# Normalising the second batch inside the first output projection of an attention and feed-forward block

## The chip, the cores and the metric

The kernel runs on one core of a Trainium2 chip. A core has five engines, each with an instruction queue of its own that runs in order: TensorE (PE, matrix products and transposes, written to PSUM), VectorE (DVE), ScalarE (ACT), GpSimd (POOL) and SyncE (SP, which here only issues DMA transfers). PE's weight loads have a row of their own (PEld). All transfers share 16 DMA engines. The metric is the device time of one execution in microseconds (us), lower is better.

## The reference

The input x has 2 batches of 1024 tokens of 1024 values; 32 query heads of 32 values share 8 key/value heads, so four query heads (a group) use one key head. The feed-forward weights are 4-bit numbers, packed eight to a word, with zero points and scales per group of 128 rows.

```python
xn = _layernorm(x, axis=-1)                     # (x - mean) / sqrt(var + 1e-5)
q, k, v = xn @ wq, xn @ wk, xn @ wv             # per head
q, k = _apply_rope(q), _apply_rope(k)           # pairs of values turned by the token's angle
attn = softmax(q @ k.T / sqrt(32) + causal mask)
s = (attn @ v) @ wo
h = silu(xn @ w_gate) * (xn @ w_up)             # w = scale * (nibble - zero - 1)
g = silu(h @ w_down)
out = x + s * g
```

## The kernel before

The work is done in five kinds of stage: for each of the two batches norm, projection, attention and output projection, and after both the feed-forward part. Everything is in fp32; a product is done as two instructions in the profile.

**Norm** (`norm`, L299). The tokens are taken in eight tiles of 128 (`t`). SP loads a tile `xt` of 512 KB, VectorE computes mean and variance (`bn_stats` twice, `bn_aggr`), ScalarE the square root (`std`), VectorE the reciprocal and the normalised `xn`; PE turns `xn` in eight 128x128 transposes into two PSUM tiles `ps_ln`, and ScalarE copies these into `xnT` (channels on partitions, tokens along the free axis). Three `xt`, three `xn` and four `ps_ln` buffers exist. The pools are opened inside the function and closed at its end.

**Projection** (`project`, L321). `turned` multiplies one 128-column weight tile with all eight channel slices of `xnT`, for each half of 512 tokens (`n`): 16 PE instructions into `ps_qk`. VectorE, POOL and ScalarE turn the result by the token angles (`cs`, `rot`) and split it into two parts, `hi` and `lo`, which SP writes to DRAM (`ks`, `qs`). First come the two key tiles `c`, each for both halves, then eight query tiles, then the values (`values`, L363) for eight token tiles. Beside the queries the row maxima of the first key head's scores are computed (`Maxima`, `head.rows()`, L477), and each channel slice of `xnT` is split and stored for the feed-forward part (`xs`). In batch 0, `look` (L209) checks and prepares the 4-bit tables in between.

**Attention** (`attend`, L554) runs under a manual schedule: the engines get its instructions in the order in which they are traced. A step is one key tile of 128 for one group `g` and one half of the queries `qb`. PE computes scores into four PSUM tiles `st`, ScalarE exponentiates them into `p`, POOL masks the diagonal tiles (`affine_select`, L636), PE multiplies `p` with the values (`o`, L655). The sums of the weights (`l`, L673) are products with ones; to save PE work POOL first adds several `p` tiles together (L757, and L783 for what is left after the last step). `groups` (L588) says which: pairs for full tiles, and all four diagonal tiles into one. The maxima of later heads are woven in by a planner with costs (`Clock`, `turn`). Query stacks live in three sets and key stacks in four, loaded by SP one or more heads ahead.

**Output projection** (`project_out`, L785). The eight weight tiles `w_o` are loaded first. For each block of 256 tokens PE computes all eight column tiles into one PSUM tile `ps_wo` of four banks (two buffers, so all eight banks). VectorE copies the first half of the columns back into `oT` and ScalarE the second half, and SP writes the block to `sT` in DRAM. Before each column tile three steps of `unpack` (L234) are traced: the 4-bit weights are loaded (`qw`, `zt`), nibbles taken apart on VectorE, turned to fp32 on ScalarE (`nf`, two buffers) and written to DRAM by POOL's queue (`ng`, 512 KB per write, 22 MB in batch 0). Steps that are left follow after the loop.

**What sets the order.** Outside attention and the down projection, the framework plans the order of each engine's queue ahead of time: by priority, which is the order of tracing, among the instructions that a model of the hardware holds ready. On the chip each queue then runs in that order and waits by semaphores. Memory for a pool is reused after earlier pools on the same stack are closed; a pool with `reuse_waits="tile"` waits for the single tiles that lay there, another for the earlier pool as a whole. The main loop over batches is at L1308.

Of the kernel before, what the change touches and what calls it, by code (L numbers as in the profile page):

```python
# [10 lines left out]
F32 = mybir.dt.float32  # L11
# [12 lines left out]
P = 128  # L24
# [12 lines left out]
def block_kernel(  # L37
# [261 lines left out]
    def norm(b, xnT):  # L299
        with tc.tile_pool(name="ln", bufs=3) as pool, tc.tile_pool(name="ln_ps", bufs=4, space=PSUM) as psp:  # L300
            for t in range(NT):
                xt = pool.tile([P, D], F32, name="xt")
                nc.sync.dma_start(xt, x[b, t * P : (t + 1) * P, :])
                stats = pool.tile([P, 2, 6], F32, name="stats")
                for h in range(2):
                    nc.vector.bn_stats(stats[:, h, :], xt[:, h * 512 : (h + 1) * 512])
                mv = pool.tile([P, 2], F32, name="mv")
                nc.vector.bn_aggr(mv, stats.rearrange("p h s -> p (h s)"))
                std = pool.tile([P, 1], F32, name="std")
                nc.scalar.activation(std, mv[:, 1:2], AF.Sqrt, bias=eps)  # L310
                rstd = pool.tile([P, 1], F32, name="rstd")
                nc.vector.reciprocal(rstd, std)
                xn = pool.tile([P, D], F32, name="xn")
                nc.vector.tensor_scalar(xn, xt, mv[:, 0:1], rstd, ALU.subtract, ALU.mult)
                for h in range(NS // 4):
                    ps = psp.tile([P, 4, P], F32, name="ps_ln")
                    for j in range(4):
                        nc.tensor.transpose(ps[:, j, :], xn[:, (4 * h + j) * P : (4 * h + j + 1) * P], ident)
                    nc.scalar.copy(xnT[:, 4 * h : 4 * h + 4, t * P : (t + 1) * P], ps)  # L319

    def project(b, xnT, qs, ks, v, side, head):  # L321


        with tc.tile_pool(name="qkv_w", bufs=3) as wp, tc.tile_pool(name="qkv", bufs=3) as pool, tc.tile_pool(
            name="qkv_t", bufs=1
        ) as tp, tc.tile_pool(name="qkv_ps", bufs=3, space=PSUM) as psp, tc.tile_pool(
            name="v_ps", bufs=2, space=PSUM
        ) as vps, tc.tile_pool(name="x_split", bufs=2) as xp:
# [5 lines left out]
            def load(w_dram, c):  # L334
                w = wp.tile([P, NS, P], F32, name="w_qk")
                nc.sync.dma_start(
                    w, w_dram.rearrange("(g p) n -> p g n", p=P)[:, :, c * P : (c + 1) * P]
                )
                return w

            def turned(w, dst, work=iter(())):
                for n in range(NB):
# [27 lines left out]

            wanted = [(wk, c) for c in range(2)] + [(wq, c) for c in range(NC)]
            loaded = [load(*wanted.pop(0)) for _ in range(2)]
            w = tp.tile([P, NS, N_KV * HD], F32, name="w_v")
            nc.sync.dma_start(w, wv.rearrange("(g p) n -> p g n", p=P))

            def following():
                if wanted:
                    loaded.append(load(*wanted.pop(0)))
                return loaded.pop(0)

            for c in range(2):
                turned(following(), ks[c])
# [55 lines left out]
    class Maxima:  # L438


        def __init__(self, qs, ks, pool, ps):
# [112 lines left out]
    def attend(head, v, oT):  # L554
# [5 lines left out]
        with ExitStack() as st:  # L560
# [27 lines left out]
            def groups(qb):  # L588
                full = [[k, k + 1] for k in range(0, qb * QB, 2)]
                return full + [list(range(qb * QB, (qb + 1) * QB))]  # L590
# [803 lines left out]
```

## Time and profile before

| | us |
|---|---|
| median of 3 runs | 2343.35 (2342.94 to 2345.72) |
| the profiled execution | 2346.94 |
| its span, first to last instruction | 2345.2 |
| PE busy | 2254.8 (96%) |
| VectorE, ScalarE, POOL busy | 1410.5, 1130.3, 801.6 |
| mean granted PE clock | 0.982 of full speed |

The stages, by PE's first and last instructions in the trace: norm of batch 0 until 32.5 us, projection until 223.6, attention until 559.4, output projection with the unpacking until 671.5, norm of batch 1 until 707.8, projection until about 890, attention until 1223.5, output projection until 1336, then the feed-forward part.

In a row of the timeline the columns are start, length, engine, line, operation, output and inputs, partitions and elements, and count; in brackets stands how long the engine was idle before it and what it waited for. In a row of stretches the columns are the stretch and its length, the busy time of PE, PEld, DVE, ACT and POOL with counts, the granted PE clock, the share of the DMA engines and GB/s. In a row of waits stand who waited for whom, the sum, the count and the longest.

### The profile page before, as it was taken

To read this page: it belongs to the slowest core of one execution; us is meant where nothing else is said; L and a number is where in the kernel's file an instruction comes from. 1 tells how busy PE (TensorE), PEld (TensorE's weight loads), DVE (VectorE), ACT (ScalarE), POOL (GpSimd) and SP (SyncE) were. 2 spreads that over 40 slices of the span, in tenths; PEclk is the share of its full clock that TensorE was granted. 3 is DMA by queue.
4 is the path that set the end of the run, shared out by engine and by line. 5 is a ranking of instruction groups with operands and counts; after the bars stand their busy time and mean duration, and the time that the engine had idled before them with its cause. 6 is when DMAs were issued, how large, how long until landed. Compare 5 with 4: busy or idle time off the path is not lost.

```text
span 2345.2 us, 30574 instructions
## 1 busy us (share of the span) xinstructions
PE 2254.8 (96%) x11265; PEld 1553.5 (66%) x11265; DVE 1410.5 (60%) x2244; ACT 1130.3 (48%) x1795; POOL 801.6 (34%) x561
## 2 busy tenths in 40 slices
PE   6999999998969999999989999999999999999987
PEld 4446555555854455555548878888877888888765
DVE  6362777762244545777722266767777677767775
ACT  3012544544332004444532365565787655556775
POOL 1421777785312325777670000000234100001352
PEclk8999999999989999999999999999999999999999
DMA  6645122105977434222029622322646645323464
GB/s 225 206 158 162 46 67 69 37 22 170 310 232 260 133 98 108 49 61 67 1 68 323 188 70 68 81 58 78 259 144 221 183 131 148 94 69 109 151 204 149
DMA packets 262342, 309.49 MB, mean 132 GB/s; under 512 B 18283, under 2 KB 202987, under 8 KB 262040
## 3 DMA queue, kind: packets, MB, share of 16 engines
q1 hardware_dynamic: 250964, 269.00, 38.5%
q0 software_dynamic: 9472, 33.83, 4.6%
q10 hardware_dynamic: 1748, 4.62, 0.7%
q8 instruction: 91, 1.49, 0.3%
q14 instruction: 67, 0.55, 0.1%
HBM read 214.58 MB, written 97.03 MB: 133 GB/s over the span
## 4 chain that ended last, share of the span: by engine, by line
PE 77%; issue 9%; POOL 8%; DVE 2%; DMA 2%; ACT 2%; SPq 0%; POOLq 0%; DVEq 0%
PE acc L1069 27%; PE acc L952 11%; PE ps_wo L799 10%; PE st L608 7%; PE s L503 7%; PE o L655 5%; PE ps_v L366 2%; PE l L673 2%; PE st L623 2%; POOL rot L353 2%; POOL rot L354 2%; PE ps_qk L346 2%; DMA xt<-in_L_attn_x 1%; POOL p L757 1%; PE s L497 1%
## 5 line engine op out<-in xcount | busy, mean ns | idle before, releaser
L1069 PE MATMUL acc<-x,w 128*128 128x512 f32 x2752 | 640.2, 393 | 1.5 <-ACT gate L1040 0.9
L1069 PEld LDWEIGHTS acc<-x,w 128*128 128x128 f32 x2752 | 512.3, 188 | 121.0 <-DVE h L1042 6.9
L513 DVE TENSOR_REDUCE mx<-s 128x1 f32<-128x512 f32 (+3 forms) x672 | 384.0, 608 | 202.0 <-PE s L503 111.3
L841 DVE TENSOR_SCALAR acc<-acc,r_gu 128x1024 f32<-128x1024 f32 x301 | 389.1, 1293 | 160.5 <-PE acc L1069 158.2
L633 ACT ACTIVATE p<-st 128x512 f32<-128x512 f32 (+3 forms) x768 | 314.7, 497 | 310.7 <-PE st L623 285.0
L839 ACT ACTIVATE acc<-acc,r_gu 128x1024 f32<-128x1024 f32 x301 | 327.5, 1088 | 230.1 <-PE acc L1069 225.2
L1053 POOL TENSOR_TENSOR h_lo<-h,h_hi 128x512 fp32r<-128x512 f32 x78 | 100.3, 1287 | 819.4 <-ACT h_hi L1052 440.5
L757 POOL TENSOR_TENSOR p<-p 128x1536 f32<-128x1536 f32 (+3 forms) x124 | 367.3, 2966 | 8.3 <-ACT p L633 6.9
L503 PE MATMUL s<-kst,qst 128*128 128x512 f32 (+3 forms) x768 | 295.0, 414 | 5.0 <-DVE mx L513 4.8
L346 PE MATMUL ps_qk<-xnT,w_qk 128*128 128x512 f32 x640 | 295.0, 603 | 0.7 <-ACT xnT L319 0.7
L841 DVE TENSOR_SCALAR acc<-acc,r_d 128x512 f32<-128x512 f32 x320 | 241.6, 759 | 67.1 <-PE acc L952 64.6
L608 PE MATMUL st<-qst,kst 128*128 128x512 f32 (+3 forms) x768 | 246.9, 379 | 5.0 <-ACT p L633 4.6
L839 ACT ACTIVATE acc<-acc,r_d 128x512 f32<-128x512 f32 x320 | 210.8, 662 | 65.6 <-PE acc L952 58.7
L952 PE MATMUL acc<-h_lo,w 128*128 128x512 f32 (+1 forms) x576 | 228.9, 397 | 2.9 <-POOL h_lo L1053 2.6
L952 PE MATMUL acc<-h_hi,w 128*128 128x512 f32 (+1 forms) x576 | 229.5, 398 | 0.7 <-ACT h_hi L1052 0.7
L799 PE MATMUL ps_wo<-oT,w_o 128*128 128x256 f32 x1024 | 224.9, 383 | 0.0
L503 PEld LDWEIGHTS s<-kst,qst 128*128 128x128 f32 x768 | 138.6, 189 | 129.9 <-DVE mx L513 68.2
L799 PEld LDWEIGHTS ps_wo<-oT,w_o 128*128 128x128 f32 x1024 | 196.7, 192 | 30.2 <-issue 2.9
L346 PEld LDWEIGHTS ps_qk<-xnT,w_qk 128*128 128x128 f32 x640 | 118.7, 192 | 123.3 <-issue 119.5
L608 PEld LDWEIGHTS st<-qst,kst 128*128 128x128 f32 x768 | 130.5, 189 | 66.5 <-ACT p L633 55.8
L655 PE MATMUL o<-p,v 128*32 128x512 f32 (+3 forms) x1536 | 164.4, 500 | 10.4 <-POOL p L636 10.4
L356 ACT CAST rot_hi<-rot 128x512 fp32r<-128x512 f32 x40 | 24.6, 617 | 269.8 <-POOL rot L354 240.3
(149 smaller groups left out, 1986.3 us busy)
## 6 DMA issues: line engine op xcount, KB each, us to landing
w<-ng SPq DMA_DIRECT2D x86, 512.0 KB, 6.0
qst<-qs SPq DMA_DIRECT2D x256, 128.0 KB, 3.9
w<-nd SPq DMA_DIRECT2D x63, 512.0 KB, 3.7
ng<-nf POOLq DMA_DIRECT2D x42, 512.0 KB, 6.1
x<-xs SPq DMA_DIRECT2D x32, 512.0 KB, 5.8
xt<-in_L_attn_x SPq DMA_DIRECT2D x16, 512.0 KB
w_qk<-in_L_attn_wq SPq DMA_DIRECT2D x16, 512.0 KB, 4.6
xs<-x_hi SPq DMA_DIRECT2D x16, 512.0 KB, 3.2
```

What stands on the lines that cost most here:

```text
L346: nc.tensor.matmul(ps, w[:, s, :], xnT[:, s, tok], start=(s == 0), stop=(s == NS - 1))
L503: nc.tensor.matmul(s[:, c * w : (c + 1) * w], q[j][:, qt * P : (qt + 1) * P], k[:, k0:k1], start=n == 1, stop=c == n - 1 and (n > 1 or not ...
L513: nc.vector.tensor_reduce(mx[:, at, js[0] : js[0] + n, k0 // TB], s[:, : w * n].rearrange("p (j t) -> p j t", j=n), AX.X, ALU.max)
L608: nc.tensor.matmul(s[:, q0:], kst[g][:, kt * P : (kt + 1) * P], stack[g][j][:, qlo + q0 : qlo + TB], start=True, stop=False,)
L633: nc.scalar.activation(p[:, j, q0:], st[j][:, q0:], AF.Exp, scale=1.0 / math.sqrt(HD))
L655: nc.tensor.matmul(o[HD * j : HD * (j + 1), q0:], v[:, kt, HD * g : HD * (g + 1)], p[:, j, q0:], start=(kt == 0), stop=last,)
L757: what(*args)
L799: nc.tensor.matmul(ps[:, c, :], ws[c][:, g, :], oT[:, g, t0 : t0 + BLK], start=(g == 0), stop=(g == NS - 1))
L839: nc.scalar.mul(a, a, r)
L841: nc.vector.tensor_scalar(a, a, r, None, ALU.mult)
L952: nc.tensor.matmul(acc[c], w[:k, c * P : (c + 1) * P], ht[:k, :], start=(f == 0 and t == 0), stop=(t == 1), skip_group_check=(f > 0),)
L1069: nc.tensor.matmul(a[:, n, :], w[i][:, g * P : (g + 1) * P], xs[t][:, g, n * TB : (n + 1) * TB], start=(g == 0 and t == 0), stop=(t == 1), ...
```

## The change

The norm becomes a generator that does one token tile at a time, with pools given by the caller. For batch 0 it runs ahead as before, now with eight `xt` buffers. For batch 1 it runs inside the output projection of batch 0: after every half of the columns of a block one tile of 128 tokens is traced, with three `xt` buffers and two `ps_ln`; the transposes are ordered behind the first half's last product. The output projection uses PSUM tiles of half the columns (two banks, three buffers), copies them by turns with VectorE and ScalarE into separate tiles `wo_r` (three buffers), and writes these to `sT` from POOL's and ScalarE's queues. `xnT` is opened before the output projection and closed before attention.

Both key tiles come as one weight `w_k` of 1 MB, loaded after the fourth token tile in batch 0 and after the last output weight for batch 1; the value weight is later loaded into the same tile. The keys are projected for the first 512 tokens (both tiles) and then for the last. In the last group's second half the four diagonal tiles are no longer added by POOL; each is summed by PE on its own. Most pools wait by tile, the first key and query stacks get a pool of their own at the bottom, and the stacks are placed in another order in memory.

```diff
-    def norm(b, xnT):
-        with tc.tile_pool(name="ln", bufs=3) as pool, tc.tile_pool(name="ln_ps", bufs=4, space=PSUM) as psp:
-            for t in range(NT):
-                xt = pool.tile([P, D], F32, name="xt")
+    def norm(b, xnT, pool, psp, bufs):
+        for t in range(NT):
+            xt = pool.tile([P, D], F32, name="xt", bufs=bufs)
...
+                nc.scalar.copy(xnT[:, 4 * h : 4 * h + 4, t * P : (t + 1) * P], ps)
+            yield
+    def load_w_at(pool, w_dram, c, **kw):
+        w = pool.tile([P, NS, P], F32, **{"name": "w_qk", **kw})
+        return w, nc.sync.dma_start(w, w_dram.rearrange("(g p) n -> p g n", p=P)[:, :, c * P : (c + 1) * P])
+    def load_kv(pool, w_dram, w=None):
+        if w is None:
+            w = pool.tile([P, NS, N_KV * HD], F32, name="w_kv")
+        nc.sync.dma_start(w, w_dram.rearrange("(g p) n -> p g n", p=P))
+        return w
...
-            for c in range(2):
-                turned(following(), ks[c])
+            for n in range(NB):
+                for c in range(2):
+                    turned(w_k[:, :, c * P : (c + 1) * P], ks[c], blocks=[n])
+            w = load_kv(None, wv, w_k)
             head.keys()
...
-            keys = [head.k] + [kp.tile([P, T], F32R, name=f"kst_{i}") for i in range(1, 4)]
+            keys = {0: head.k, **{i: kp.tile([P, T], F32R, name=f"kst_{i}") for i in (1, 3, 2)}}
...
-            sets = [head.q] + [[qp.tile([P, T], F32R, name=f"qst_{i}_{j}") for j in range(NREP)] for i in (1, 2)]
+            sets = {0: head.q, **{i: [qp.tile([P, T], F32R, name=f"qst_{i}_{j}") for j in range(NREP)] for i in (2, 1)}}
...
-            def groups(qb):
+            def groups(g, qb):
                 full = [[k, k + 1] for k in range(0, qb * QB, 2)]
-                return full + [list(range(qb * QB, (qb + 1) * QB))]
+                diag = list(range(qb * QB, (qb + 1) * QB))
+                return full + ([[k] for k in diag] if g == NKV - 1 and qb == NB - 1 else [diag])
...
-                    n = len(groups(qb)) - 1 - groups(qb).index(grp)
+                    n = min(2, len(groups(g, qb)) - 1 - groups(g, qb).index(grp))
...
-                    at(end + 4 - n, total, hd, hd["p"], span(qb, grp[0]), grp[0] == 0, last)
+                    at(max(i + 3, end + 4 - n), total, hd, hd["p"], span(qb, grp[0]), grp[0] == 0, last)
...
-    def project_out(b, oT, side, turns):
+    def project_out(b, oT, side, turns, xnT, xp):
         BLK = 256
+        HC = NC // 2
+        with ExitStack() as st:
+            wp = st.enter_context(tc.tile_pool(name="wo", bufs=NC, reuse_waits="tile"))
+            res = st.enter_context(tc.tile_pool(name="wo_out", bufs=3, reuse_waits="tile"))
+            psp = st.enter_context(tc.tile_pool(name="wo_ps", bufs=3, space=PSUM, reuse_waits="tile"))
+            following = iter(())
+            if xnT is not None:
+                ln = st.enter_context(tc.tile_pool(name="ln", bufs=3, reuse_waits="tile"))
+                ln_ps = st.enter_context(tc.tile_pool(name="ln_ps", bufs=2, space=PSUM, reuse_waits="tile"))
+                following = norm(b + 1, xnT, ln, ln_ps, 3)
+            loads = [load_w_at(wp, wo, c, name="w_o") for c in range(NC)]
+            ws = [w for w, _ in loads]
+            w_k = None
+            if xp is not None:
+                with tc.issue_after(loads[-1][1].ins):
+                    w_k = load_kv(xp, wk)
+            first = None
             for t0 in range(0, T, BLK):
...
+                for h in range(2):
+                    ps = psp.tile([P, HC, BLK], F32, name="ps_wo")
+                    for c in range(HC):
+                        for _ in range(turns):
+                            next(side, None)
+                        for g in range(NS):
+                            mm = nc.tensor.matmul(
...
+                    first = first or mm
+                    with tc.issue_after(first.ins):
+                        next(following, None)
+                    r = res.tile([P, HC, BLK], F32, name="wo_r")
+                    copy, queue = ((nc.vector.tensor_copy, nc.gpsimd), (nc.scalar.copy, nc.scalar))[h]
+                    copy(r, ps)
+                    queue.dma_start(sT_dram[b][:, HC * h : HC * (h + 1), t0 : t0 + BLK], r)
+            return w_k
...
+    x_open, xnT, xp = open_x()
+    with tc.tile_pool(name="ln", bufs=3) as ln, tc.tile_pool(name="ln_ps", bufs=4, space=PSUM) as ln_ps:
+        for t, _ in enumerate(norm(0, xnT, ln, ln_ps, NT)):
+            if t == NT // 2 - 1:
+                w_k = load_kv(xp, wk)
     for b in range(B):
...
+            room = [q0p.tile([P, T], F32R, name=f"st_{j}") for j in range(1 + NREP)]
...
+                x_open.close()
                 attend(head, v, oT)
+        if b == B - 1:
+            ffn_args = start_ffn(ffn_open)
+            xnT = xp = None
+        else:
+            x_open, xnT, xp = open_x()
+        with tc.tile_pool(name="unpack", bufs=2, side="right", reuse_waits="tile") as up:
+            side = unpack(up, b)
+            w_k = project_out(b, oT, side, 3, xnT, xp)
+            for _ in side:
+                pass
```

## The prediction

> **What bounds the kernel now.** I read the page's engine rows and slices first, then busy time by stretch, then the chain of waits and the engines' timelines around the places that the change touches.
>
> ```profile
> PE 2254.8 (96%) x11265; PEld 1553.5 (66%) x11265; DVE 1410.5 (60%) x2244; ACT 1130.3 (48%) x1795; POOL 801.6 (34%) x561
> ```
> TensorE (PE) is busy for 96% of the span, so a gain must come from the 90 us in which it is idle or at a low clock. Stretches (span of the stretch, then PE, PEld, DVE, ACT, POOL busy, PE clock, DMA share, GB/s):
>
> ```profile
> 24.00:28.00 4.00, 1.69 (x8) 1.29 (x7) 2.87 (x7) 1.95 (x4) 0.00 (x0) 0.73 1.09 321
> 672.00:680.00 8.00, 0.00 (x0) 0.00 (x0) 0.74 (x1) 2.29 (x2) 0.00 (x0) 0.67 0.98 278
> 700.00:704.00 4.00, 1.92 (x10) 1.55 (x9) 3.02 (x8) 1.66 (x4) 0.00 (x0) 0.50 0.00 0
> 559.40:615.60 56.20, 56.20 (x258) 49.28 (x255) 19.17 (x57) 23.13 (x24) 18.92 (x22) 0.98 0.91 276
> 615.60:671.40 55.80, 55.80 (x260) 49.03 (x259) 12.45 (x38) 22.97 (x24) 20.13 (x26) 1.00 0.95 286
> ```
> The two norms (first three rows) leave PE idle at half clock. Beside the first output projection (last two) PE has no idle time, VectorE is idle 72% and ScalarE 59% of it, but the DMA engines are 91 to 95% busy with the unpacking. PE's timeline at the end of attention, in the second norm and at the first product:
>
> ```profile
> 32.50 27.94 PE L346 MATMUL ps_qk<-xnT,w_qk 128*128 128x512 f32 x60 [0.68 <-ACT xnT L319]
> 550.30 1.08 PE L655 MATMUL o<-p,v 128*32 128x256 f32 x8 [3.75 <-POOL p L636]
> 551.16 1.94 PE L673 MATMUL l<-p,ones_f 128*32 128x512 f32 x8
> 558.07 1.42 PE L673 MATMUL l<-p,ones_f 128*32 128x512 f32 x8 [2.84 <-POOL p L783]
> 684.80 3.65 PE L318 MATMUL ps_ln<-ident,xn 128*128 128x128 f32 x16 [13.09 <-DVE rstd L312]
> 707.78 5.48 PE L366 MATMUL ps_v<-w_v,xnT 128*128 128x256 f32 x14 [0.68 <-ACT xnT L319]
> ```
> And the chain of waits, where one group of 16 product instructions at full clock can be read:
> ```profile
> 671.90 10.32 DMA xt<-in_L_attn_x
> 713.26 6.87 PE ps_qk L346 x16
> ```
> Last, how far ScalarE runs behind PE in the output projection, by its PSUM copies, and why:
> ```profile
> 629.41 0.99 ACT L805 COPY oT<-ps_wo 128x1024 f32<-128x1024 f32 x1
> 668.20 0.99 ACT L805 COPY oT<-ps_wo 128x1024 f32<-128x1024 f32 x1
> ACT nf L259 <- DMA ng<-nf: 56.5, 19, 6.0
> ```
> A block of 256 tokens takes PE 28.0 us (112.0 / 4), so blocks 2 and 3 were complete at 615.5 and 643.5; their copies came 13.9 and 24.7 us later, because they stand in ScalarE's queue behind unpack conversions that wait for `ng` writes. PE doesn't feel it: it has two block buffers.
>
> **The second norm moved.** Between the end of the output projection (671.5) and the first key product (713.1) pass 41.6 us. Of PE's work there 64 transposes move into the projection, at 27.7 / 128 = 0.216 us each (page's group of L318): 13.8 us. The 14 value instructions of 707.78 come back at the end of the stage at full rate, 24.62 / 114 = 0.216 each: 3.0 us. What goes is 41.6 - 13.8 - 3.0 = **24.8 us**: the wait for x (10.3 us behind the last unpack writes), the VectorE chain, and the half clock.
>
> What moves with it: eight x loads and a 1 MB key weight on SP's queue, past the unpack's qw and zt loads, some 0.4 us of issue each, hidden as SP is mostly waiting. x3 to x7 wait for a buffer of three, which gives them about three halves (42 us) of lead over their transposes; even the 10.3 us landing fits. Per tile VectorE takes 1.29 + 0.21 + 0.15 + 0.81 = 2.5 us, 20 us in all, and ScalarE 8 x (0.3 + 1.2) + 1.3 table load = 13 us; both fit the idle time. The writes of sT leave SP for POOL (0.9 us each by its `ng` issues) and ScalarE's queue. The new `wo_r` buffers add a wait of copies for the sT write three halves earlier: 42 us against a landing of 11.0 us, so nothing, unless ScalarE is over 30 us late. The value weight now waits on SP for the last key product, with the rotated keys' writes behind it; it is needed over 120 us later. I put these at nothing.
>
> **What takes its place.** The transposes stand in PE's queue between two halves, and all later products stand behind them. They wait for two PSUM tiles (`ln_ps` has two buffers, one tile of tokens needs both), so transposes of tile i+1 wait until ScalarE has copied tile i, 14.0 us of PE time earlier. But ScalarE's queue is 13.9 us late at the middle and 24.7 us at three quarters. With 14 us of tolerance the stall is 24.7 - 14.0 = 10.7 us if the lag stays as it was; the lag grew by 10.8 us in 28, and if the planner puts the unpack 15.7 us (one half and its transposes) later, it reaches 24.7 + 6.1 = 30.8 and the stall 16.8. I take the middle, **13.8 us**, since more DMA traffic (5.2 MB at 281 GB/s is 18 us) speaks for growth and the earlier loads of w_o (below) against it. The ends are 0 (the planner orders norms ahead of conversions) and 60 (third rival).
>
> A stall also costs clock. After the idle 1.1 us at 225.2 PE ran at 0.50 from 228 to 234, and after the 2.84 us at 555.2 until 562. Inside the stall that only lets ScalarE catch up; after the last one about 4 us at half rate are lost, **2.0 us**.
>
> The Trainium skill, TensorE: Matmul & The Clock Gate, section Why this matters for your kernels, says the clock is kept as long as no idle gap exceeds some 3 us. The rows above show drops after shorter gaps; by the rule three stalls of under 3 us each would cost no clock, and the forecast would be 2 us lower.
>
> **The start.** Before, the first key product starts at 32.5, after all eight tiles; the fourth group ends at 32.5 + 9.07 (chain; half clock) + 3 x 6.87 = 62.2. After, eight x buffers let all loads go at once. The first lands at 4.3 (first VectorE work); 512 KB at the 320 to 370 GB/s seen from 24 to 32 us is 1.6 us, so tile 3 lands near 9 and w_k near 12.5. VectorE then sets the pace: tile 3 leaves it at 4.3 + 4 x 2.5 + 0.9 (round trip to ScalarE) = 15.2, transposes and copy about 2.2: the first product at 17.4. PE then owes four groups (27.5), 32 transposes (6.9) and 2.2 for the half clock: 54.0. Tile 7 leaves VectorE at 25, in time. Gain **8.2 us**. If the first group's PSUM bank is only free after the last tile, it starts at about 27.3 and ends at 57.0: 5.2. With no half clock: 10.4. A loss has no mechanism here: the same loads come earlier; 0 is the floor.
>
> **The tails of attention.** Of the three POOL sums over the diagonal p tiles of the last head (3.45 + 2.36 + 1.27 us) none is left; PE gets three more groups of `l` (384, 256, 128 columns). The first tail still starts at 550.3, behind the 4.51 us POOL sum of a full pair. Then at half clock o 0.86, l 1.71, l 1.71 to 554.6, and at full clock 0.89 + 0.66 + 0.21 + 0.44 + 0.22: 557.0 instead of 559.4, and 2.6 us at half clock behind it (1.3 us) are gone: 3.7. The second tail, from 1213.9, ends at 1220.1 instead of 1223.5, and 1.4 of clock: 4.8. Sum 8.5, floor 0 (a late w_o); I take **8.0**. Those output weights now lie first on the query set last used by head 6, so part of their 4 MB can land before 545, out of the busy stage.
>
> **Half columns** in the second output projection: PE waited 0.52 us at 1338.2 for ScalarE's copy, which waited for VectorE's of the same tile. Separate tiles: **0.5**. Key order, memory order of stacks and the finer waits elsewhere: PE lost under 6 us in the first projection (0.81 + 1.96 + 1.41 + 1.53), to row maxima, which the change leaves as they are: 0.
>
> **Sum.** 24.8 + 8.2 + 8.0 + 0.5 - 13.8 - 2.0 = 25.7 us. The profiled execution took 2346.94 us (span 2345.2), 3.6 above the median of 2343.35; from it the sum gives 2321.2, from the median 2317.7. I forecast 2318.
>
> **Rivals.** (1) No coupling: norms and copies stay ahead of ScalarE's lag, nothing for stalls and clock: 25.7 + 15.8 = 41.5, so 2302. For: the idle time of VectorE and ScalarE; against: the 24.7 us lag. (2) The start doesn't move, since the first group waits for the last tile or for w_k, and the tails give only half: 2343.35 - (24.8 + 4 + 0.5 - 15.8) = 2330. For: DMA and VectorE are full there; against: the first group has no use for tiles 4 to 7. (3) Slower: VectorE's queue waits for x inside the unpack. Each x took 10.3 us to land at 671.9 where about 5 are usual (4.92 for the next); if each of eight holds the nibble work 5.4 us, ScalarE's lag grows by 43, the stall to 57. Then 41.5 - 57 - 2 = -17.5: 2361. It decides when the stall passes 39.5 us, 2.9 times my value. For: DMA at 95%; against: loads with three buffers of lead.
>
> **Chances.** My forecast (2308 to 2324) 0.45; rival 1 0.22; rival 2 0.15; rival 3 0.13; between it and rival 2, within 0.2% (4.7 us, about what can be told from no change), 0.05. So faster 0.82, same 0.05, slower 0.13. The range runs from rival 1 with the best start, 2300, to a stall of 30 us with rival 2's start, 2339.
>
> **What would show it.** First product L346 near 17 instead of 32.5; no PE wait for POOL L783; no idle time between ps_wo and ps_qk of batch 1; waits of ps_ln in the output projection put down to ScalarE's xnT copies, 14 us in sum; PE in that stage 112 + 14 busy. I am wrong if those waits are missing or pass 30 us, or if the unpack's tail holds the rotations afterwards.

## The result, and the profile after

The changed kernel takes 2349.68 us (median of 14 runs, 2346.70 to 2353.04) against 2343.14 us of the kernel before (14 runs beside them, 2340.69 to 2345.97): a ratio of 1.0027, 95% interval 1.0019 to 1.0035. It is slower by 0.27%, where 2318 us was forecast. The two profiled executions lie apart from these medians on opposite sides (before 2346.94 us, above all 14; after 2347.66 us, near the lowest; span 2345.9), so that the traces have to explain a loss of 0.7 us, not of 6.5. Against the forecast gain of 25.7 us, 26 us are missing by the traces and 32 by the medians. One execution of one run below, the one with the old tail, is left out of its ratio: it took 3634.33 us, at a mean granted clock of 0.556.

PE's row of the page after, and its group for the output projections, which had no idle time before (columns: busy, mean ns, idle ahead of it and what ended most of that):

```profile
PE 2249.7 (96%) x11313; PEld 1550.2 (66%) x11313; DVE 1410.3 (60%) x2244; ACT 1131.3 (48%) x1797; POOL 795.5 (34%) x563
L822 PE MATMUL ps_wo<-oT,w_o 128*128 128x256 f32 x1024 | 227.7, 384 | 23.5 <-DMA w_o<-in_L_attn_wo 23.5
```

The new wait is 23.5 us for the output weights. PE's timeline after, at the start, in the first output projection, and in the second:

```profile
27.49 27.77 PE L354 MATMUL ps_qk<-xnT,w_kv 128*128 128x512 f32 x64
...
548.86 3.72 PE L822 MATMUL ps_wo<-oT,w_o 128*128 128x256 f32 x16
...
630.78 1.97 PE L318 MATMUL ps_ln<-ident,xn 128*128 128x128 f32 x8 [8.48 <-ACT xnT L319]
649.93 1.14 PE L318 MATMUL ps_ln<-ident,xn 128*128 128x128 f32 x8 [2.02 <-ACT xnT L319]
669.94 1.97 PE L318 MATMUL ps_ln<-ident,xn 128*128 128x128 f32 x8 [5.06 <-ACT xnT L319]
686.98 27.63 PE L354 MATMUL ps_qk<-xnT,w_kv 128*128 128x512 f32 x64
```
```profile
1194.16 1.08 PE L665 MATMUL o<-p,v 128*32 128x256 f32 x8 [3.74 <-POOL p L646]
1200.96 3.72 PE L822 MATMUL ps_wo<-oT,w_o 128*128 128x256 f32 x16
1205.68 7.17 PE L822 MATMUL ps_wo<-oT,w_o 128*128 128x256 f32 x32 [1.00 <-DMA w_o<-in_L_attn_wo]
1235.04 102.60 PE L822 MATMUL ps_wo<-oT,w_o 128*128 128x256 f32 x464 [22.18 <-DMA w_o<-in_L_attn_wo]
1337.29 3.12 PE L1100 MATMUL acc<-x,w 128*128 128x512 f32 x12
```

Up to 1200.96 the change gains about what was forecast: the second output projection starts 22.55 us earlier than before (1223.51). Then PE does 48 of its 512 product instructions and stands for 22.18 us. The feed-forward part starts at 1337.29, before at 1335.97. In the stretches of that stage after, PE is empty while the DMA engines are fully busy (columns as in the forecast's rows of stretches):

```profile
1205.68:1212.85 7.17, 7.17 (x32) 6.00 (x32) 0.00 (x0) 0.00 (x0) 0.00 (x0) 1.00 1.00 384
1212.85:1235.04 22.19, 0.01 (x2) 0.01 (x1) 0.00 (x0) 0.00 (x0) 0.00 (x0) 0.56 1.09 364
1235.04:1337.30 102.26, 102.26 (x465) 89.62 (x465) 19.36 (x52) 26.75 (x27) 13.45 (x16) 0.98 0.66 206
```

What the DMA engines carried is on SP's queue. Before:

```profile
1185.85 24.62 SPq L791 DMA_DIRECT2D w_o<-in_L_attn_wo  x5
1226.42 14.50 SPq L819 DMA_DIRECT2D x<-xs  x16
1241.92 8.89 SPq L810 DMA_DIRECT2D w<-ng  x3
1250.87 5.21 SPq L791 DMA_DIRECT2D w_o<-in_L_attn_wo  x3
```

And after, with SP's longest wait in that stretch:

```profile
1079.52 122.03 SPq L327 DMA_DIRECT2D w_o<-in_L_attn_wo  x3
1203.86 13.91 SPq L850 DMA_DIRECT2D x<-xs  x16
1218.73 8.94 SPq L841 DMA_DIRECT2D w<-ng  x3
1227.72 8.82 SPq L327 DMA_DIRECT2D w_o<-in_L_attn_wo  x5
```
```profile
SPq L327 <- PE l L683: 120.8, 1, 120.8
```

The first of these rows merges three loads: the first is issued at 1079.5, and SP then waits 120.8 us, until attention's last product with the values `v` ends at 1200.4, before it issues the second and third. The loads behind them wait in the same queue. There the 16 transfers of x for the feed-forward part (8 MB) and three of its weights (1.5 MB) come next, and the other five output weights only from 1227.72. Before, five of the eight had been issued ahead of x. In the built program of after, the buffers of the second and third weight lie on `v`, which attention reads until its last product; before, `v` lay below the weights and shared no byte with them. The traces show no addresses, but they fit: the last scores, which read the key and query stacks, end at 1189.5, so the stacks are not what SP waits for until 1200.5. The first output projection shows the same wait without the harm: SP issues one weight at 504.1, waits 44.2 us and issues the other seven from 548.4, but there no x goes ahead of them, and PE waits only 0.33 us.

### The profile page after: what moved, and what is told of

It reads as the page before. It is cut to its first block, busy times and chain, and to the rows that moved or that the text cites. A ratio compares the mean times of both kernels' runs of the same rounds, so it can differ in the third digit from the quotient of the medians.

```text
span 2345.9 us, 30638 instructions
## 1 busy us (share of the span) xinstructions
PE 2249.7 (96%) x11313; PEld 1550.2 (66%) x11313; DVE 1410.3 (60%) x2244; ACT 1131.3 (48%) x1797; POOL 795.5 (34%) x563
## 4 chain that ended last, share of the span: by engine, by line
PE 72%; issue 9%; POOL 8%; DMA 5%; ACT 2%; DVE 2%; SPq 1%; ACTq 0%; POOLq 0%; DVEq 0%
PE acc L1100 27%; PE acc L983 12%; PE s L510 7%; PE st L618 7%; PE o L665 5%; PE ps_wo L822 5%; PE l L683 3%; POOL rot L361 2%; PE st L633 2%; POOL rot L362 2%; DMA ng<-nf 2%; PE ps_v L374 1%; PE ps_qk L354 1%; POOL p L767 1%; PE s L504 1%
## 5 line engine op out<-in xcount | busy, mean ns | idle before, releaser
L767 POOL TENSOR_TENSOR p<-p 128x2048 f32<-128x2048 f32 (+3 forms) x122 | 360.3, 2958 | 8.3 <-ACT p L643 6.9
L822 PE MATMUL ps_wo<-oT,w_o 128*128 128x256 f32 x1024 | 227.7, 384 | 23.5 <-DMA w_o<-in_L_attn_wo 23.5
L354 PE MATMUL ps_qk<-xnT,w_qk 128*128 128x512 f32 x512 | 237.6, 600 | 0.0
L665 PE MATMUL o<-p,v 128*32 128x512 f32 (+3 forms) x1536 | 164.1, 499 | 10.4 <-POOL p L646 10.4
L354 PEld LDWEIGHTS ps_qk<-xnT,w_qk 128*128 128x128 f32 x512 | 93.7, 191 | 91.4 <-issue 88.9
L646 POOL TENSOR_SCALAR_AFFINE_SELECT p<-p 128x512 f32<-128x512 f32 x128 | 80.9, 638 | 168.3 <-ACT p L643 168.1
L361 POOL TENSOR_TENSOR rot<-rot,cs 128x512 f32<-128x512 f32 x40 | 54.0, 1350 | 246.8 <-DVE rot L360 219.2
L510 PE MATMUL s<-kst,qst 128*128 128x512 f32 (+3 forms) x384 | 136.1, 386 | 0.0
L983 PEld LDWEIGHTS acc<-h_lo,w 128*128 128x128 f32 (+1 forms) x576 | 108.4, 188 | 30.7 <-POOL h_lo L1084 5.2
```

The costliest lines, as they stand in the source:

```text
L354: nc.tensor.matmul(ps, w[:, s, :], xnT[:, s, tok], start=(s == 0), stop=(s == NS - 1))
L510: nc.tensor.matmul(s[:, c * w : (c + 1) * w], q[j][:, qt * P : (qt + 1) * P], k[:, k0:k1], start=n == 1, stop=c == n - 1 and (n > 1 or not ...
L665: nc.tensor.matmul(o[HD * j : HD * (j + 1), q0:], v[:, kt, HD * g : HD * (g + 1)], p[:, j, q0:], start=(kt == 0), stop=last,)
L767: what(*args)
L822: mm = nc.tensor.matmul(ps[:, c, :], ws[HC * h + c][:, g, :], oT[:, g, t0 : t0 + BLK], start=(g == 0), stop=(g == NS - 1),)
L983: nc.tensor.matmul(acc[c], w[:k, c * P : (c + 1) * P], ht[:k, :], start=(f == 0 and t == 0), stop=(t == 1), skip_group_check=(f > 0),)
```

## The experiments

Each was run beside the kernel before, on the same chip; ratios are to that. The first two ask for the cause of the 22 us.

**x behind the output weights.** The change with one difference: the loads of x and of the first feed-forward weights are traced and issued behind the last output weight.

```diff
+            if x_loads:
+                with tc.issue_after(loads[-1][1].ins):
+                    x_loads()
             first = None
             for t0 in range(0, T, BLK):
...
-            w_k = project_out(b, oT, side, 3, xnT, xp)
+            w_k = project_out(b, oT, side, 3, xnT, xp, x_loads if b == B - 1 else None)
```

> The changed kernel, with the loads of x and of the first feed-forward weights traced after the eight output weights and ordered behind the last of them on SP. Theory A, SP's order: PE's 22.18 and 1.00 us of idle time in the second output projection shrink to 1 to 2 us in sum and some 2 us of half clock behind them go too, so 2349.7 - 24 = about 2325, and the stage starts and ends as in the kernel before but 22 us earlier. Theory B, half columns or DMA bandwidth: with half columns PE needs four weights in a row, and 4 MB of weights beside 8 MB of x come too late in any order; then over 10 us of the wait stay and the time is 2338 or more.

Measured: 2324.41 us, ratio 0.9919 (0.9902 to 0.9935). SP's queue and PE in this run:

```profile
1081.27 131.20 SPq L327 DMA_DIRECT2D w_o<-in_L_attn_wo  x8
1212.84 18.06 SPq L853 DMA_DIRECT2D x<-xs  x16
```
```profile
SPq L327 <- PE o L665: 120.4, 1, 120.4
```
```profile
1207.26 107.32 PE L825 MATMUL ps_wo<-oT,w_o 128*128 128x256 f32 x496 [0.78 <-DMA w_o<-in_L_attn_wo]
```

The weights' buffers still come free only at the end of attention (SP's wait is here put down to `o`, the product that reads `v`), but 7 loads without x ahead of them land in time: of 23.2 us of waits 0.78 are left, and the run is 25 us faster than the change (by the difference of the ratios, 0.0108 of 2343). So theory B, half columns or too little bandwidth, falls.

**v below the weights.** The other half of the mechanism: x stays where the change has it, but `v` gets a pool that stays open through the output projection, so that no weight buffer lies on it (and the key stacks are placed in plain order).

```diff
+        qp = keep_open.enter_context(tc.tile_pool(name="qkv_T", bufs=1, reuse_waits="tile"))
         with tc.tile_pool(name="at_q0", bufs=1, reuse_waits="tile") as q0p, tc.tile_pool(
             name="at_first", bufs=1, reuse_waits="tile"
-        ) as fp, tc.tile_pool(name="qkv_T", bufs=1, reuse_waits="tile") as qp:
+        ) as fp:
...
-            keys = {0: head.k, **{i: kp.tile([P, T], F32R, name=f"kst_{i}") for i in (1, 3, 2)}}
+            keys = {0: head.k, **{i: kp.tile([P, T], F32R, name=f"kst_{i}") for i in (1, 2, 3)}}
```

> The changed kernel, with the order of traced loads untouched, but the value tile v kept below the first stacks in memory and open through the output projection (as in the kernel before), and key stacks placed 1, 2, 3. Theory A goes back to memory: the second and third of the eight weight buffers lie on v, which is read until the last step of attention, and the other five wait behind them on SP, until x is ready and goes first. With v elsewhere only the row tiles hold weights back, until about 1189 by the changed kernel's clock; all eight are issued by 1200, before x (1203.9). Then the 23 us of waiting go without any edit of the loads: about 2324. If memory has nothing to do with it, SP's order stays and the time too: 2350.

Measured: 2320.61 us, ratio 0.9906 (0.9889 to 0.9922).

```profile
1075.89 113.28 SPq L327 DMA_DIRECT2D w_o<-in_L_attn_wo  x6
1200.82 13.15 SPq L850 DMA_DIRECT2D x<-xs  x16
1214.93 10.49 SPq L841 DMA_DIRECT2D w<-ng  x3
1225.47 4.89 SPq L327 DMA_DIRECT2D w_o<-in_L_attn_wo  x2
```
```profile
1197.92 110.77 PE L822 MATMUL ps_wo<-oT,w_o 128*128 128x256 f32 x512
```

Not all eight weights come ahead of x, as the expectation had it, but six, and six are enough: PE runs 512 instructions without a wait, and the last two weights land while it works on the others. The wait for the end of attention is gone: the sixth load is issued by 1189.2, when the row tiles come free. So it is the place of `v` in memory that made the loads late, and the order of the queue behind it that made the lateness cost 22 us. Taking away either is enough. The placement of the key stacks was changed along with `v` and not tested alone; but the last scores end 11 us before the wait does, so the stacks can't be what held the loads.

**Copies on VectorE.** The next four runs ask what sets the waits in the first output projection, 15.6 us in the change. This one moves the copies of the turned second batch from ScalarE to VectorE, beside x behind the weights.

```diff
-                nc.scalar.copy(xnT[:, 4 * h : 4 * h + 4, t * P : (t + 1) * P], ps)
+                (nc.vector.tensor_copy if b else nc.scalar.copy)(xnT[:, 4 * h : 4 * h + 4, t * P : (t + 1) * P], ps)
```

> The kernel of e1 with the transposes of the second norm copied to xnT by VectorE instead of ScalarE. In the first output projection of the changed kernel PE waits 8.48 + 2.02 + 5.06 = 15.6 us for ScalarE's xnT copies. Theory: the copies stand behind unpack conversions that wait for ng writes; VectorE's queue is less late there (10.0 and 17.8 us at the middle and at three quarters in the kernel before, against 13.9 and 24.7), so 17.8 - 14.0 = some 4 us of waiting remain, 3 to 8: about 10 us less than e1, 2315. Rival: PE waits because x or the whole unpack is late, whichever engine copies: within 2 us of e1.

Measured: 2324.33 us, ratio 0.9919 (0.9903 to 0.9936), the same as without. PE's waits are 2.13 + 6.16 + 4.13 + 1.32 = 13.7 us, now put down to VectorE, against 14.7. The theory that ScalarE's queue is the late one falls: VectorE's stands behind the same unpacking.

**Four buffers for the unpacked tiles.** On top of v below the weights, four `nf` in place of two.

```diff
-            nf = pool.tile([P, 4, 2, 2 * P], F32R, name="nf")
+            nf = pool.tile([P, 4, 2, 2 * P], F32R, name="nf", bufs=4 if b == 0 else 2)
```

> The run with v below the weights, and four buffers instead of two for the unpacked tiles nf in the first output projection. There ScalarE waited 42 us for stores of nf to leave (ACT nf <- DMA ng<-nf, 15 times) and VectorE 31 us for nf behind it. Theory 'buffers': the lag is that of two buffers; with four, ScalarE's copies are on time, TensorE's 12.5 us of waits fall to about 4, and the time is about 2313. Theory 'traffic': the stores drain at what the DMA engines carry, four buffers only let the queue run two tiles further ahead; waits stay within 10 to 14 us and the time within 2318 to 2322.

Measured: 2335.95 us, ratio 0.9966 (0.9952 to 0.9980): 14 us slower, which neither theory had. PE's waits rise from 12.5 to 27.6 us:

```profile
599.92 1.94 PE L318 MATMUL ps_ln<-ident,xn 128*128 128x128 f32 x8 [6.09 <-DVE xn L314]
619.47 1.63 PE L318 MATMUL ps_ln<-ident,xn 128*128 128x128 f32 x8 [3.26 <-ACT xnT L319]
654.35 1.97 PE L318 MATMUL ps_ln<-ident,xn 128*128 128x128 f32 x8 [18.29 <-ACT xnT L319]
```

The largest goes back to an input tile. POOL issues eight writes (4 MB) in one stretch, and the tile asked for at 634.96 is there for VectorE only at 651.05. POOL, SP and VectorE:

```profile
621.84 7.09 POOL L267 DMA_DIRECT2D ng<-nf  x8
```
```profile
634.96 2.73 SPq L303 DMA_DIRECT2D xt<-in_L_attn_x  x2
```
```profile
651.05 1.29 DVE L306 BATCH_NORM_STATS2 stats<-xt 128x6 f32<-128x512 f32 x2 [11.19 <-DMA xt<-in_L_attn_x]
```

More buffers let more writes pile up ahead of the one load that PE's order depends on. The median landing time of an `ng` write rises from 6.0 us with two buffers to 9.1 with four.

**Two steps and one step of the unpacking per column**, both with v below the weights.

```diff
-                        for _ in range(turns):
+                        for _ in range(turns if xnT is None else 2):
```

> The run with v below the weights, and in the first output projection two steps of the unpacking per column instead of three (its 110 steps then reach over 55 of the 64 columns, not 37). With v below, the first output projection still holds TensorE's waits for the copies of the turned batch, 8.1 us on xn and 4.4 us on xnT, 12.5 in all. Theory 'order': the copies are late because they stand behind unpacking steps in the queues of ScalarE and VectorE; with fewer steps ahead of each the waits fall to about 4 us, and the time goes from 2320.6 to about 2313. Theory 'traffic': the window from 545 to 690 us holds about 41 MB at 282 GB/s with the DMA engines 0.93 to 0.97 busy, so that a wait taken from the copies comes back at the end, where the rest of the unpacking stands before the next projections: 2319 to 2324.

> The run with v below the weights, with one step of the unpacking per column of the first output projection instead of three (two gave 9.3 us of waits and 2316.9, three 12.5 and 2320.6). Only 64 of its 110 steps then stand between the columns, 46 behind the last. Theory: the waits for copies follow the share of the unpacking's traffic that lies ahead of them; with 64 steps, some 13 of 22 units, the DMA engines are busy 0.7 of the stage and the waits fall under 3 us, but the other 9 units, 4.3 us each, stand in ScalarE's and VectorE's queues ahead of the rotations of the next keys and queries: 39 us, of which three projections' buffers hide perhaps 10; about 20 us slower than two steps, 2337. Rival: the units left go by beside the projections, as their 50 us from 690 to 740 have room (DMA 0.84, VectorE 0.4 busy): 2308 to 2312.

Measured: two steps 2316.85 us, ratio 0.9887 (0.9870 to 0.9903), waits 5.59 + 3.66 = 9.3 us; one step 2316.02 us, ratio 0.9883 (0.9867 to 0.9900), waits 4.55 + 3.20 = 7.8 us, both again put down to `xnT`. Both are 4 to 5 us better than three steps, at the edge of what the intervals tell apart. The large loss expected of one step did not come, since the source's pace is not the queue's: the framework plans the queue. With three steps the copies of the fourth turned tile stand behind 24 conversions on ScalarE, with two or one behind 23, and the last conversion starts at 674.8, 675.0 and 673.5. The conversions with one step:

```profile
L259 ACT ACTIVATE nf<-nib x44: 613/1042/1079, 565.4 to 673.5; 128x1024 fp32r<-128x1024 uint8 x42, 128x512 fp32r<-128x512 uint8 x2
```

The place of the copies in ScalarE's queue thus hardly moved, and these two runs don't test whether an earlier place there would help.

**The norm put back** behind the first output projection, the rest as in the run with x behind the weights.

```diff
-            w_k = project_out(b, oT, side, 3, xnT, xp, x_loads if b == B - 1 else None)
+            w_k = project_out(b, oT, side, 3, None, None, x_loads if b == B - 1 else None)
...
+        if b == 0:
+            with tc.tile_pool(name="ln", bufs=3) as ln, tc.tile_pool(name="ln_ps", bufs=4, space=PSUM) as ln_ps:
+                for t, _ in enumerate(norm(1, xnT, ln, ln_ps, 3)):
+                    if t == NT // 2 - 1:
+                        w_k = load_kv(xp, wk)
```

> The run with x issued behind the output weights (2324.4), with the second norm put back behind the first output projection; start, tails, half columns and order of keys stay as in the change. Theory, with the prediction's term: the gap between the output projection and the first key product (25 us with nothing on TensorE but the 64 transposes) comes back and the 14.7 us of waits for copies go, so 10 to 11 us slower: about 2335. Rival: the waits are the price of the traffic and not of the norm, they stay or come back elsewhere: 25 us slower, 2349. Other rival: the move is worth nothing net: 2324.

Measured: 2346.66 us, ratio 1.0012 (1.0002 to 1.0022), 22 us slower than with the norm moved, twice what the theory said and close to the first rival's 25. PE, then SP:

```profile
549.02 3.72 PE L825 MATMUL ps_wo<-oT,w_o 128*128 128x256 f32 x16
553.06 107.32 PE L825 MATMUL ps_wo<-oT,w_o 128*128 128x256 f32 x496 [0.32 <-DMA w_o<-in_L_attn_wo]
679.82 4.64 PE L318 MATMUL ps_ln<-ident,xn 128*128 128x128 f32 x24 [19.44 <-DVE rstd L312]
697.15 1.94 PE L318 MATMUL ps_ln<-ident,xn 128*128 128x128 f32 x8 [12.68 <-DVE mv L308]
708.37 22.10 PE L354 MATMUL ps_qk<-xnT,w_kv 128*128 128x512 f32 x48
```
```profile
660.41 2.30 SPq L303 DMA_DIRECT2D xt<-in_L_attn_x  x3
684.41 2.00 SPq L327 DMA_DIRECT2D w_qk<-in_L_attn_wq  x3
686.52 13.13 SPq L303 DMA_DIRECT2D xt<-in_L_attn_x  x5
```

The projection starts 10.4 us earlier than in the kernel before (559.42) and needs 111.4 us, but its unpacking is not done earlier: the last conversion starts at 674.5 us, before at 667.7. The first product of the next batch comes at 708.37, before at 707.78. So all that start and tail had gained is lost between the two, by two waits with different causes. The 19.44 us are the unpacking: the first tile of x is on VectorE at 665.49, but its `std` comes on ScalarE only at 677.88, behind the last conversions, which wait for `ng` writes. The 12.68 us are mostly SP's queue again, in a way that the kernel before doesn't have: SP stands 21.5 us until a write of `wo_r` has landed, ahead of three query weights, and the fourth tile of x behind them is issued at 686.52, though its buffer was free when the first `xn` was done, at 679.7. By our estimate some 7 us of the 22 (686.52 - 679.7) are thus this run's own queue order and not the place of the norm; the 15 that are left are still more than the theory's 10 to 11. With the norm inside, PE has work until the unpacking is done.

**The kernel before with single sums** only. It asks from the other side what a gain ahead of the unpacking is worth.

```diff
-            def groups(qb):
+            def groups(g, qb):
                 full = [[k, k + 1] for k in range(0, qb * QB, 2)]
-                return full + [list(range(qb * QB, (qb + 1) * QB))]
+                diag = list(range(qb * QB, (qb + 1) * QB))
+                return full + ([[k] for k in diag] if g == NKV - 1 and qb == NB - 1 else [diag])
...
```

> The kernel before, with the four diagonal tiles of the last head's second half summed one by one on PE, and nothing else. If this part works by itself, the two tails are shorter by 2.2 and 2.8 us (the changed kernel's distances from the first o product of the tail to the first output product, 6.96 and 6.80 instead of 9.12 and 9.62) and lose 2.7 us less by half clock: 2343.1 - 7.7 = 2335.5. If the output weights, whose last load was issued at 551.9, now hold PE instead, half of that: 2339.

Measured: 2339.71 us, ratio 0.9983 (0.9973 to 0.9993). That is the rival's 2339, but not for its reason: no output weight holds PE in the trace (which is of the slowest of the ten executions, 2345.44 us). The first output projection starts 2.54 us earlier, at 556.88 instead of 559.42, and PE then waits 15.95 us for x at the norm (before 13.09), so that the next batch's first product comes only 0.81 us earlier, at 706.97; the second tail is 7.08 us long instead of 9.62, and its projection takes 110.77 us where it took 112.80.

**The old tail** on the run with x behind the weights.

```diff
-                return full + ([[k] for k in diag] if g == NKV - 1 and qb == NB - 1 else [diag])
+                return full + [diag]
```

> The run with x issued behind the output weights (2324.4, 18.5 below the kernel before), with the last head's sums of the diagonal taken from one group again. Theory: each tail gets back what the change took from it, 9.12 - 6.96 = 2.2 us in the first and 9.62 - 6.80 = 2.8 in the second, 5.0 together: 2329 to 2330, 13.5 below before. Rival, by the traffic of the first output projection: the first tail's 2.2 us fall into the waits for copies that follow it, and only the second tail's 2.8 count: about 2327. Prediction's term of 8.0: 2332.

Measured: ratio 0.9929 (0.9909 to 0.9948) against 0.9919 with single sums, three executions of 2325.56 to 2332.23 us. The intervals overlap, so the time alone does not tell the three cases apart. In the trace the tails are 8.77 and 8.86 us long, 1.7 and 1.9 longer than with single sums.

**Three input buffers in the first norm**, and **the old order of the keys**, each alone on the run with x behind the weights.

```diff
-        for t, _ in enumerate(norm(0, xnT, ln, ln_ps, NT)):
+        for t, _ in enumerate(norm(0, xnT, ln, ln_ps, 3)):
```

> The run with x issued behind the output weights (2324.4), with three input buffers instead of eight for the first norm, as before the change; the order of the keys by first tokens stays. Theory: the earlier first key product (27.5 against 32.5 us) and the full clock of the keys come from the eight buffers that let all tokens load at once; without them 7 us slower, about 2331. Rival: the gain is that of the keys' order alone: 2324 to 2326.

```diff
-            for n in range(NB):
-                for c in range(2):
+            for c in range(2):
+                for n in range(NB):
                     turned(w_k[:, :, c * P : (c + 1) * P], ks[c], blocks=[n])
```

> The run with x issued behind the output weights, with the key products of both batches in the old order again (all tokens of one column tile, then the other); the eight input buffers and the one load of the key weights stay. With three buffers instead of eight 2.4 of the 6.6 us went that the first scores of attention start earlier than before the change (229.8 to 223.2). Theory: the rest, some 4 us, is the order's, since the first product of the first 512 tokens needs half the turned batch only: 2328. Rival: all 64 transposes stand ahead of the keys in TensorE's order either way, so that the order of the keys is worth nothing: 2324 to 2325.

Measured: three buffers 2330.35 us, ratio 0.9941 (0.9925 to 0.9958), 5 us slower; old order 2323.64 us, ratio 0.9917 (0.9900 to 0.9933), no difference. PE at the start, with the old order:

```profile
24.61 3.65 PE L318 MATMUL ps_ln<-ident,xn 128*128 128x128 f32 x16 [2.08 <-DVE rstd L312]
28.05 27.80 PE L354 MATMUL ps_qk<-xnT,w_kv 128*128 128x512 f32 x64
```

The eight buffers carry the gain at the start and the order of the keys nothing, as all 64 transposes stand ahead of the first key product either way. With three buffers the first products of the row maxima within attention come at 225.57 us, before the change at 229.83, so 4.3 us of the gain at the start stay without them. With eight buffers they come at 221.61 to 223.20, run by run, so that the start accounts for 2.4 to 4.0 of the 5 us. What carries the other 4.3 was not settled: the single load of the key weights was not undone alone, nor were buffers and order undone together.

**All that helped.** v below, x behind the weights and two steps per column, each as above.

> All that helped together: v below the weights, x issued behind the output weights, two steps of the unpacking per column. Theory: with v below, TensorE no longer waits for an output weight though x goes ahead of the last two, so that x's place adds nothing: 2316 to 2318. Rival: x's 8 MB out of the way of the weights is worth the 1 to 2 us of short waits left: 2314 to 2316.

Measured: 2317.57 us, ratio 0.9891 (0.9875 to 0.9908): x's place adds nothing once the weights don't lie on `v`. The best version is thus the change with `v` below the weights and one or two steps per column, 1.1 to 1.2% faster than the kernel before.

## Why the prediction was wrong

The forecast's terms, read between the same marks of the two traces (positive is gain, in us):

| term | forecast | measured | from |
|---|---|---|---|
| start | 8.2 | 8.0 | first product of the row maxima within attention, 229.83 to 221.82 |
| tails, with the clock behind them | 8.0 | 8.3 | 2.16 + 2.82 shorter; projections of 112.06 and 112.80 us go to 110.77 without waits |
| norm moved, less waits for copies and clock | 9.0 | 7.9 | start of the first to start of the second projection, 664.09 to 652.10, less 2.82 and 1.29 of the tails |
| half columns | 0.5 | 0 | first wait of the feed-forward part, 0.52 to 0.57 (the one for `oT` is gone, one for `acc` is in its place) |
| memory order, SP's queue | 0 | -25.9 | second projection 136.33 us, with v below 110.42 |
| rest (attention 0.4, feed-forward part 0.6) | 0 | 1.0 | |

The sum is -0.7, the difference of the two spans. By the medians the change loses 5.8 us more than these two traces show; with `v` below the weights it is 28 us faster (by the difference of the ratios, 0.0121 of 2343), against the 25.9 of the table.

**The step that failed** is the one that put the loads of the output weights at nothing and below: "Those output weights now lie first on the query set last used by head 6, so part of their 4 MB can land before 545, out of the busy stage", and "memory order of stacks ... : 0". The first buffer does come free early, and in the first projection one weight of eight is issued before 545. But the second and third lie on `v`, and SP's queue is in order, so that the five behind them wait for it too. With `v` elsewhere six loads are issued by 1189.2, 8.7 us before the output projection starts. The prediction counted the moves on SP in issue time (0.4 us each) and asked of each load whether it was needed soon. It did not ask, for each buffer, what lies in its place and when that is last read, nor what else becomes ready for the same queue in the meantime. Those were the x loads of the feed-forward part, whose lines the change doesn't touch.

**Right, with its size.** The waits for the copies of the turned batch came where and as forecast: three, put down to `xnT`, 15.6 us against 13.8. That the size came so close is in part luck, as 13.8 was the middle between 10.7 and 16.8. Their cause in the prediction, ScalarE behind the conversions, was only the near end of it: VectorE is as late, and with two steps, one step or four buffers the last conversion still starts at 673.5 to 675.9 us. What is common to all is the DMA engines: in the stretch from 605 to 665 us after they are 0.99 to 1.01 busy.

```profile
605.00:635.00 30.00, 21.52 (x99) 18.71 (x98) 12.29 (x34) 14.62 (x19) 11.40 (x13) 0.84 1.01 322
635.00:665.00 30.00, 27.86 (x131) 23.85 (x130) 9.49 (x29) 12.98 (x14) 11.79 (x14) 0.99 0.99 301
```

That the traffic sets the waits is argued from this and from the run with four buffers; no run with less traffic was made.

**Right in sum, wrong in mechanism: the start.** The first product was to come at 17.4 and came at 27.49, the case given with 5.2 us; it still gained 8.0, since 64 instructions then take 27.77 us at a clock of 0.86 in the first microsecond and 1.00 behind it, where 0.50 had been forecast. All 64 transposes stand ahead of the first key product in PE's queue; whether the PSUM bank that the prediction names for that case is the reason, no run shows. That 8.0 meets the forecast's 8.2 is luck.

**The rivals.** None gave the right reason. The slower one (2361) had VectorE wait for x inside the unpacking, decisive from a stall of 39.5 us; the stall was 15.6. The loss came from the other output projection, which the prediction had only counted for its half columns. Without it the forecast stands: with `v` below the weights the change takes 2320.61 us, forecast 2318, likeliest range 2308 to 2324.

**Slips of arithmetic and reading** that didn't decide. The upper end of the range, 2339, doesn't come out of its own terms: a stall of 30 us and no gain at the start leave 24.8 + 8.0 + 0.5 - 30 - 2.0 = 1.3 us, so 2342. And the 90 us from which a gain was to come are idle time alone; what PE loses at a low clock lies in its busy time.

## What to carry to other kernels

When a change moves pools, ask of every buffer that is loaded ahead what lay in its place and when that is last read; the latest of them holds every later load of the same in-order queue, here 5 weights of 512 KB behind a wait of 120.8 us. The wait alone need not cost anything: in the first output projection PE lost 0.33 us by it. Ask then what becomes ready for that queue meanwhile and is issued first: 9.5 MB that nobody needed for 100 us cost PE 22 us. And work gained ahead of a stage that is full of transfers can be lost in the wait behind it, unless something fills PE until the transfers are done: with single sums alone 2.54 us ahead of the unpacking became 0.81 behind it, and with the norm put back 10.4 us became nothing, in part by a queue of that run's own.

## What was not expected of the hardware

Deeper buffering made a stage with busy DMA engines slower: four `nf` instead of two took the median landing of an `ng` write from 6.0 to 9.1 us, one input tile's landing to about 16 us, and PE's waits from 12.5 to 27.6 us.

PE's clock in the stretches after waits of different length, in the trace after (the waits ahead of them: 8.48, 2.02 and 5.06 us; the clock is the third figure from the end):

```profile
630.78:634.00 3.22, 3.22 (x12) 2.95 (x13) 0.48 (x1) 1.46 (x3) 0.91 (x1) 0.50 1.00 291
649.93:653.00 3.07, 3.07 (x18) 2.77 (x19) 1.40 (x4) 1.42 (x3) 2.58 (x3) 1.00 1.00 302
669.94:673.00 3.06, 3.06 (x12) 2.83 (x13) 1.57 (x5) 3.06 (x4) 1.37 (x2) 0.52 0.58 189
```

The wait of 2.02 us left the clock at 1.00, those of 5.06 and 8.48 us halved it. These rows agree with the rule that the prediction weighed (the Trainium skill, TensorE: Matmul & The Clock Gate, section Why this matters for your kernels: no idle gap over some 3 us). Of the prediction's two rows against it one falls: the clock had been at 0.50 since the wait of 3.75 us at 550.3, ahead of the one of 2.84. The drop after 1.1 us at 225.2 stays unexplained; the trace after has it too (1.12 us idle at 217.7, clock 0.58 from 222 to 224).
